# A four-layer graph network on one core: adjacency blocks transposed by DMA, and a reordered first stage

## The chip, the core and the metric

The kernel runs on one core of one Trainium2 chip. Such a core has a matrix engine, TensorE (PE in the profile; its weight loads, PEld, overlap its products), a vector engine (DVE), a scalar engine (ACT), GpSimd (POOL) and SyncE (SP), which here only issues DMAs. ACT and POOL can issue DMAs too; all of them share the core's 16 DMA rings. Every engine works through its own instructions in order and waits for the others by semaphores. The metric is the device time of one execution in microseconds.

## The reference

A node matrix x (3327 x 512) passes four layers that share one adjacency matrix (3327 x 3327, 0/1 integers). Layers 0 to 2 are attention layers with 8, 4 and 8 heads, layer 3 averages over neighbours. Cut to layer 0:

```python
h = jnp.maximum(_layernorm(x, axis=-1), 0.0)
Wh = jnp.einsum('nd,hdo->hno', h, W)                 # 8 heads of 64
f1 = jnp.einsum('hno,ho->hn', Wh, a1)
f2 = jnp.einsum('hno,ho->hn', Wh, a2)
e = leaky_relu(f1[:, :, None] + f2[:, None, :], 0.2)
e = jnp.where(adj[None] > 0, e, NEG_INF)
out = elu(einsum('hnm,hmo->hno', softmax(e, -1), Wh))
x = x + out                                           # heads side by side
```

## The kernel before

Rows are cut into 26 tiles of 128 (the last has 127 rows). Since exp(leaky_relu(f1 + f2)) is a product of a row factor and a column factor on each side of the sign of f1 + f2, attention becomes products of 0/1 matrices with the projected rows, scaled by column factors. For each head and each block of columns a 0/1 matrix "f1 + f2 > 0" is made (`gt`), cut with the adjacency (`tht` = gt AND mask, then `gt` = mask without tht), and both multiply the **pieces** (`ab`): the scaled projected rows, each split into three bf16 parts. The columns come in five groups, `JG` = 6, 6, 6, 4 and 4 blocks of 128. The rows come in seven **chunks** of four tiles (the last of two).

*The first stage* (lines 820 to 847) projects all 26 tiles for layer 0. Tile by tile, `node_stages` gives stages that `Hooks.run` advances by one for each tile in flight: x is loaded, its statistics are taken on DVE, three small steps on POOL end the norm (`norm`), ACT makes the relu (`normed`); PE transposes it and ACT copies it out of PSUM (`transposed`, L137 and L141, tile `hT`); PE projects it (`projected`, L388); ACT and DVE scale and split it (`scaled`, `pieces`); SP stores the pieces to DRAM. The score vectors a1 and a2 are folded into further columns of the weight tile first (`fold`, L299 and L303, half of its products on POOL). From the fifth step on, each step also makes one **mask** (`load_mask`), 20 of them in this stage: POOL loads a 128-row strip of one column group of the adjacency with a cast to bf16 (`at`, L216); PE transposes its blocks into PSUM (`tp`, L221); DVE turns them into 0 or 2 in fp8 (`st`, L225), and SP stores them to DRAM (L230). They are in DRAM since all layers read them again.

*Attention of a layer* (`attention`) runs over the chunks and, for each, over the heads. SP loads the row scores (`s1b`, L624) and the pieces (`ab`, L601: seven buffers, five groups a head); ACT compares 128x512 blocks (L656), DVE some others (L653); DVE makes `tht` and `gt` (L662, L666); PE multiplies in two passes of two row tiles each (L694, L697); DVE reduces. After each pass `hooks.run` lets further work in: the steps of the next layer's tiles, and in layer 0 one or two of the 110 masks that are left. One head before a chunk ends, the masks of the next must be done; SP loads them (L238).

Instructions are placed by a scheduler: on each engine those that are ready go by the order of the program. `after(inst, name)` adds an order to that, without a semaphore. The PSUM tiles `tp` (two buffers) are shared by the masks' transposes and by `transposed`.

Of the kernel before, what the change touches and what calls it, by code (L numbers as in the profile page):

```python
# [52 lines left out]
def tile_gnn(ctx: ExitStack, tc: tile.TileContext, x, adj, W0, a01, W1, al, ar, W2, a2,  # L53
# [95 lines left out]
    stored = {}  # L149
    gone = []  # L150
# [52 lines left out]
    def load_mask(pool, t, g):  # L203


        hooks.done += 1
        n = pn(t)
        c, k = where[t]
        j0, nj = JG[g]
        w = min(nj * P, N - j0 * P)  # L210
        at = pool.tile([P, JM * P], BF16, name="at", bufs=3)
        if n < P:
            nc.vector.memset(at, 0.0)
        elif w < nj * P:
            nc.vector.memset(at[:, w:nj * P], 0.0)
        ld = nc.gpsimd.dma_start(at[:n, :w], adj[t * P:t * P + n, j0 * P:j0 * P + w])  # L216
        if gone:
            after(ld, gone[-2] if len(gone) > 1 else stored[NT - 1])
        tp = ps.tile([P, 8, P], BF16, name="tp", bufs=2)
        for j in range(nj):  # L220
            tr = nc.tensor.transpose(tp[:, j, :], at[:, j * P:(j + 1) * P], identb)  # L221
            if j == 0 and gone:
                after(tr, gone[-1])
        st = pool.tile([P, JM, P], FP8, name="st", bufs=3)
        nc.vector.tensor_scalar(st[:, :nj], tp[:, :nj], 0.0, 2.0, op0=ALU.is_gt, op1=ALU.mult, saturate=False)  # L225
        if j0 <= t < j0 + nj:
            d = pool.tile([P, P], BF16, name="d", bufs=1)
            nc.vector.tensor_tensor(d, tp[:, t - j0, :], negI, ALU.is_gt)
            nc.vector.tensor_scalar(dg1[:, t, :], d, 2.0, None, op0=ALU.mult, saturate=False)
        nc.sync.dma_start(maskd[c][g][:, k], st[:, :nj])  # L230

    def mask_tiles(c, self_loops=False, early=False):
        t0, nt = chunks[c]
        tiles, loops = [], []
        for g, (j0, nj) in enumerate(JG):
            m = mk.tile([P, PER * JM * P], FP8, name="m")
            v = m[:, :nt * nj * P].rearrange("p (k j i) -> p k j i", k=nt, j=nj)
            ld = nc.sync.dma_start(v, maskd[c][g])  # L238
            if early and c == 0:
                after(ld, stored[21])  # L240
            if self_loops:
                for k in range(nt):
                    if j0 <= t0 + k < j0 + nj:
                        loops.append((v[:, k, t0 + k - j0, :].bitcast(U32), dg1[:, t0 + k, :].bitcast(U32)))
            tiles.append(v)
        if self_loops != "later":
            set_loops(loops)
        return (tiles, loops) if self_loops == "later" else tiles
# [14 lines left out]
    def open_layer(l):  # L263
# [17 lines left out]
        for i in range(2):  # L281
            av.append(pre.tile([P, 2, H2, DK], F32, name="h"))
            ld = nc.sync.dma_start(av[i].rearrange("p f h d -> p (f h) d"), a_srcs[l][i].partition_broadcast(P))
            if l:
                after(ld, stored["gate"])
        for k in range(KC):
            for f in range(2):
                dst = L.w[:, k, f, :D // 2]
                if l == 0:
                    nc.sync.dma_start(dst.rearrange("p (g o) -> p g o", g=H2),  # L290
                                      W0[f * H2:(f + 1) * H2, k * P:(k + 1) * P, :].rearrange("h p o -> p h o"))
                else:
                    W = (W1, W2)[l - 1]
                    ld = nc.sync.dma_start(dst, W[k * P:(k + 1) * P, f * (D // 2):(f + 1) * (D // 2)])
                    if l:
                        after(ld, stored["gate"])
        def fold(i, k):
# [3 lines left out]
            if gone:  # L301
                after(m, gone[-1])
            nc.vector.tensor_reduce(L.w[:, k, :, D // 2 + i * H2:D // 2 + (i + 1) * H2], pr, AX.X, ALU.add)  # L303
        folds = [lambda i=i, k=k: fold(i, k) for i in range(2) for k in range(KC)]
        if l:
            hooks.small = folds
        else:
            for f in folds:
                f()
# [18 lines left out]
    def normed(xt, mv, pool, behind=None):  # L328
        h = pool.tile([P, D], F32, name="h", bufs=2)
        act = nc.scalar.activation(h, xt, AF.Relu, bias=mv[:, 3:4], scale=mv[:, 2:3])  # L330
        if behind:
            after(act, behind)
        return h
# [7 lines left out]
    def pieces(L, t, AB, pool, first, behind=None):  # L341
# [32 lines left out]
        elif first and o == two - 1:  # L374
            stored[t] = nc.sync.dma_start(abd[l][g][:, :, js, :].rearrange("h p j w -> p h j w"), pt).ins.name
# [3 lines left out]
    def projected(L, t, hT, first):  # L379
# [4 lines left out]
        pws = []  # L384
        for f in range(2):
            pw = (accs if first else ps).tile([P, D // 2 + H], F32, name="acc" if first else "mm")
            for k in range(KC):
                L.mm = nc.tensor.matmul(pw, hT[:, k, :], L.w[:, k, f, :], start=(k == 0), stop=(k == KC - 1)).ins.name  # L388
# [3 lines left out]
            pws.append(pw)  # L392
# [84 lines left out]
    def node_stages(L, t, get_x, pool, first=False):  # L477
# [30 lines left out]
        if first:  # L508
            return [lambda: (q.update(x=get_x()), statistics(), relu()), turn,
                    lambda: parts(L, t, scaled(L, t, projected(L, t, q["hT"], first), pool, first), pool, first), send]  # L510
# [82 lines left out]
    ahead = {}  # L593

    def load_pieces(L, pool, g, h):
# [4 lines left out]
        v = tl[:, :nj * HW].rearrange("p (j w) -> p j w", j=nj)  # L600
        return v, nc.sync.dma_start(v, abd[L.l][g][h])  # L601

    def attention(L, hooks, open_next, close):
# [4 lines left out]
        masks = mask_tiles(0, l == 1, l == 0)  # L608
        for c, (t0, nt) in enumerate(chunks):
            W = nt * P  # L610
# [3 lines left out]
            for h in range(H):  # L614
# [8 lines left out]
                s1b = rp.tile([P, WMAX], F32, name="s1b", bufs=2)  # L623
                nc.sync.dma_start(s1b[:, :W].rearrange("p (k i) -> p k i", k=nt), s1d[l][t0:t0 + nt, h, :].partition_broadcast(P))  # L624
                ab = []
                for a in range(2 if l == 1 else 1):
                    row = []
                    for g, (_, nj) in enumerate(JG):
# [6 lines left out]
                        else:  # L635
                            v, ld = ahead.pop(g) if g in ahead else load_pieces(L, mp if l else bp, g, h)
# [5 lines left out]
                s1v = s1b[:, :W].rearrange("p (k i) -> p k i", k=nt)  # L642
                th, flip = [[], []], []
                for g, (j0, nj) in enumerate(JG):

                    pt = mp.tile([P, PER * JM * P], FP8, name="tht", bufs=10 if l == 1 else 7)
                    gt = pt if l == 1 else mp.tile([P, PER * JM * P], FP8, name="gt", bufs=7)
                    gv = gt[:, :nt * nj * P].rearrange("p (k j i) -> p k j i", k=nt, j=nj)
                    pv = pt[:, :nt * nj * P].rearrange("p (k j i) -> p k j i", k=nt, j=nj)
                    for jj in range(nj):  # L650
                        j = j0 + jj
                        if j in GP_ON_DVE[l]:
                            nc.vector.tensor_scalar(gv[:, :, jj, :], s1v, L.ns2[:, j, h:h + 1], 2.0,  # L653
                                                    op0=ALU.is_gt, op1=ALU.mult, saturate=False)
                        else:
                            nc.scalar.activation(gv[:, :, jj, :], s1v, AF.Relu, bias=L.ks2[:, j, h:h + 1], scale=BIG,  # L656
                                                 saturate=False)
                    flat = "p k j i -> p (k j i)"
                    mu = masks[g].rearrange(flat).bitcast(U32)
                    gu = gt[:, :nt * nj * P].bitcast(U32)  # L660
                    pu = pt[:, :nt * nj * P].bitcast(U32)
                    nc.vector.tensor_tensor(pu, gu, mu, ALU.bitwise_and)  # L662
                    if l == 1:
                        flip.append((pu, mu))
                    else:
                        nc.vector.tensor_tensor(gu, pu, mu, ALU.bitwise_xor)  # L666
                    th[0].append(pv)
                    th[1].append(gv)
# [109 lines left out]
    def load_x(l, t, pool, *name, behind=None):  # L778
# [7 lines left out]
        if behind:  # L786
            after(ld, behind)
# [32 lines left out]
    with tc.tile_pool(name="first", bufs=1) as fp:  # L820
# [5 lines left out]
        def first_x(t, lead=6):  # L826

            while len(xa) < min(NT, t + lead):
# [4 lines left out]
                nc.sync.dma_start(xt[:pn(u)], x_rows(0, u))  # L833
# [5 lines left out]
        hooks.masks = [lambda t=t, g=g: load_mask(ip, t, g) for t in range(NT) for g in range(len(JG))]  # L839
        hooks.tiles = [node_stages(L, t, lambda t=t: first_x(t), fp, True) for t in range(NT)]  # L840
        n = 0
        while hooks.tiles or hooks.flying:
            hooks.run(1, 0, 1 if n >= 4 and hooks.done < 20 else 0)
            for g, (j0, nj) in enumerate(JG[:-1]):
                if n == j0 + nj + 2:
                    ahead[g] = load_pieces(L, bp, g, 0)
            n += 1
    A, R = [("A", D, F32, n) for n in A_BUFS], ("R", PER * 2 * 129, F32, 1)
    ab, gt, tht = ("ab", JM * 400, BF16, 7), ("gt", PER * JM * P, FP8, 7), ("tht", PER * JM * P, FP8, 7)
    tags = [[A[0], R, tht, ("gap", 15 * 1024, FP8, 1), gt],  # L850
            [A[1], ("ab", JM * 258, F32R, 7), R, ("ts", 2 * JM * P, F32R, 3), ("tv", 2 * 4 * P, F32R, 2), tht[:3] + (10,)],
            [A[2], ab, ("R", PER * 2 * 65, F32, 1), tht, gt]]
    hooks.masks = [lambda t=t, g=g: load_mask(ip, t, g) for t in range(NT) for g in range(len(JG))][hooks.done:]
# [531 lines left out]
```

## Time and profile before

| | us |
|---|---|
| four timed runs | 3610.37, 3605.89, 3600.28, 3607.64 |
| their median | 3606.77 |
| the profiled execution | 3605.24 |
| its span, first to last instruction | 3603.3 |
| PE busy | 3466.8 (96%) |
| DVE, ACT, POOL busy | 2648.8, 2511.2, 602.3 |
| first attention product of layer 0 starts | 180.92 |
| last adjacency transposes start | 990.6 |

Line numbers (L221) are those of the kernel before. A busy time is the sum of an engine's records; matmuls are pipelined, so that a record of 0.25 us may follow another after 0.08 us, and what a matmul costs is read from the distance of starts. A wait is an engine's idle time, with the instruction that ended it. The ring share is the mean busy share of the 16 DMA rings. SPq lines are DMAs that SP issues. Durations come from one profiled execution, of which only the order and the distances are used.

### The profile page before, as it was taken

How to read it: one execution, taken by the hardware profiler on the slowest of the kernel's cores; microseconds unless marked ns; L12 is line 12 of the kernel's file. 1: busy time of each engine (PE TensorE's matmuls, PEld its weight loads, DVE VectorE, ACT ScalarE, POOL GpSimd, SP SyncE). 2: the span in 40 equal slices, each digit the busy share in tenths (PEclk: the TensorE clock that was granted, in tenths of full speed). 3: DMA queues.
4: the chain of work that ended last, by engine and by line, in shares of the span. 5: the costliest groups of instructions: out<-in, count | busy, mean ns of one | idle time of the engine just before them, and what ended most of it. 6: DMA issues, size and time to landing. Idle time of an engine off the chain costs nothing. (4 is left out here: it accounts for less than half of the span.)

```text
span 3603.3 us, 78551 instructions
## 1 busy us (share of the span) xinstructions
PE 3466.8 (96%) x31291; PEld 3129.6 (87%) x31291; DVE 2648.8 (74%) x5227; ACT 2511.2 (70%) x4113; POOL 602.3 (17%) x855
## 2 busy tenths in 40 slices
PE   6799999999999999999999989999999999999998
PEld 5599999999999878888888869989898989876886
DVE  6698888888887779888888868867676768672211
ACT  5688787777787788888798767767676767572111
POOL 6501221111110111233222230001010101010000
PEclk9899999999999999999999999999999999999999
DMA  7688787788766877877777876655555555576331
GB/s 211 220 237 229 202 230 210 220 220 234 228 205 208 283 274 262 288 253 276 279 259 271 312 268 201 195 178 183 176 187 182 172 176 189 167 271 253 102 104 52
DMA packets 369431, 780.69 MB, mean 217 GB/s; under 512 B 35906, under 2 KB 207333, under 8 KB 368416
## 3 DMA queue, kind: packets, MB, share of 16 engines
q1 hardware_dynamic: 341024, 713.17, 59.5%
q0 software_dynamic: 28032, 62.41, 7.2%
q8 instruction: 249, 4.08, 0.4%
q14 instruction: 126, 1.03, 0.1%
HBM read 667.96 MB, written 129.64 MB: 221 GB/s over the span
## 5 line engine op out<-in xcount | busy, mean ns | idle before, releaser
L694 PE MATMUL acc<-ab,tht 128*128 128x195 bf16 (+1 forms) x10816 | 1840.1, 248 | 14.9 <-DVE tht L662 13.6
L697 PE MATMUL acc<-ab,gt 128*128 128x195 bf16 (+1 forms) x10816 | 1839.1, 248 | 6.5 <-DVE rc L734 3.9
L656 ACT ACTIVATE gt<-s1b,ks 128x512 fp8e4<-128x512 f32 (+1 forms) x2464 | 1457.3, 677 | 315.3 <-issue 158.5
L694 PEld LDWEIGHTS <-tht 128*128 128x128 fp8e4 x10816 | 1059.0, 98 | 28.2 <-DVE tht L662 15.2
L697 PEld LDWEIGHTS <-gt 128*128 128x128 fp8e4 x10816 | 1058.7, 98 | 26.5 <-issue 19.8
L662 DVE TENSOR_TENSOR tht<-gt,m 128x768 uint32<-128x768 uint32 (+3 forms) x560 | 446.7, 798 | 141.5 <-ACT gt L656 139.5
L666 DVE TENSOR_TENSOR gt<-tht,m 128x768 uint32<-128x768 uint32 (+3 forms) x560 | 450.1, 804 | 8.7
L590 ACT CAST ts<-tht 128x1536 fp32r<-128x1536 fp8e4 x208 | 300.1, 1470 | 59.0 <-PE acc L687 55.7
L687 PE MATMUL acc<-ab,ts 128*128 128x258 f32 x2496 | 334.1, 290 | 4.6 <-ACT ts L590 3.4
L653 DVE TENSOR_SCALAR gt<-s1b,ns 128x512 fp8e4<-128x512 f32 (+1 forms) x448 | 221.9, 500 | 148.7 <-PE acc L697 147.5
L687 PEld LDWEIGHTS acc<-ab,ts 128*128 128x128 f32 x2496 | 313.9, 190 | 13.6 <-ACT ts L590 3.8
L921 PE MATMUL acc<-y,mf 128*128 128x512 f32 x1352 | 309.8, 391 | 1.6 <-DVE mf L916 1.6
L656 ACT ACTIVATE tht<-s1b,ks 128x512 fp8e4<-128x512 f32 (+1 forms) x504 | 308.5, 681 | 2.8 <-DMA s1b<-s 2.3
L921 PEld LDWEIGHTS acc<-y,mf 128*128 128x128 f32 x1352 | 253.5, 188 | 57.8 <-DVE mf L916 2.0
L712 DVE TENSOR_REDUCE R<-acc 128x130 f32<-128x390 f32 x416 | 214.2, 554 | 91.8 <-PE acc L697 91.2
L797 POOL TENSOR_TENSOR xt<-xt,e 128x512 f32<-128x512 f32 x72 | 123.2, 1711 | 888.9 <-DVE e L796 578.8
L690 PE MATMUL acc<-ab,tht 128*128 128x387 bf16 x1248 | 225.8, 329 | 7.6 <-DMA ab<-ab 4.8
L918 ACT CAST mf<-m 128x768 fp32r<-128x768 fp8e4 (+1 forms) x78 | 59.1, 762 | 245.1 <-PE acc L921 233.3
L687 PE MATMUL acc<-ab,tv 128*128 128x258 f32 x1664 | 219.4, 283 | 2.7 <-DVE R L708 0.9
L687 PEld LDWEIGHTS acc<-ab,tv 128*128 128x128 f32 x1664 | 207.3, 189 | 5.1 <-DVE tv L590 1.6
L388 PE MATMUL mm<-w,hT 128*128 128x260 f32 (+1 forms) x832 | 199.0, 393 | 9.9 <-ACT hT L141 6.2
L690 PEld LDWEIGHTS <-tht 128*128 128x128 fp8e4 x1248 | 117.3, 98 | 84.7 <-DMA ab<-ab 5.2
(141 smaller groups left out, 3412.1 us busy)
## 6 DMA issues: line engine op xcount, KB each, us to landing
ab<-ab SPq DMA_DIRECT2D x336, 600.0 KB, 5.6
ab<-ab SPq DMA_DIRECT2D x224, 400.0 KB, 4.0
ab<-ab SPq DMA_DIRECT2D x112, 774.0 KB, 6.2
ab<-ab SPq DMA_DIRECT2D x112, 516.0 KB, 5.4
ab<-ab SPq DMA_DIRECT2D x56, 582.0 KB, 6.1
s1b<-s SPq DMA_DIRECT2D x120, 256.0 KB, 6.1
m<-mask SPq DMA_DIRECT2D x72, 384.0 KB, 4.0
ab<-pt SPq DMA_DIRECT2D x13, 1600.0 KB, 7.6
```

The costliest lines, as they stand in the source:

```text
L388: L.mm = nc.tensor.matmul(pw, hT[:, k, :], L.w[:, k, f, :], start=(k == 0), stop=(k == KC - 1)).ins.name
L590: (nc.scalar.copy if KIND[g] == "s" else nc.vector.tensor_copy)(t[:, :k1 - k0, :nj], th[a][g][:, k0:k1])
L653: nc.vector.tensor_scalar(gv[:, :, jj, :], s1v, L.ns2[:, j, h:h + 1], 2.0, op0=ALU.is_gt, op1=ALU.mult, saturate=False)
L656: nc.scalar.activation(gv[:, :, jj, :], s1v, AF.Relu, bias=L.ks2[:, j, h:h + 1], scale=BIG, saturate=False)
L662: nc.vector.tensor_tensor(pu, gu, mu, ALU.bitwise_and)
L666: nc.vector.tensor_tensor(gu, pu, mu, ALU.bitwise_xor)
L687: mm = nc.tensor.matmul(acc[k][:, :2 * DA], thr[g][:, k - ks[0], jj, :], ab[a][g][:, jj, :], start=(j == 0), stop=(j == NT - 1), skip_grou ...
L690: mm = nc.tensor.matmul(acc[k][:, :3 * DA], th[a][g][:, k, jj, :], ab[a][g][:, jj, :3 * DA], start=(j == 0), stop=(j == NT - 1), skip_grou ...
L694: nc.tensor.matmul(acc[k][:, :3 * DA + o], th[0][g][:, k, jj, :], ab[0][g][:, jj, :3 * DA + o], start=(j == 0), stop=False, skip_group_che ...
L697: mm = nc.tensor.matmul(acc[k][:, AO:AO + 3 * DA + o], th[1][g][:, k, jj, :], ab[0][g][:, jj, AO:AO + 3 * DA + o], start=False, stop=(j == ...
L712: nc.vector.tensor_reduce(R[:, k], v.rearrange("p a (s d) -> p a d s", s=3), AX.X, ALU.add)
L921: nc.tensor.matmul(acc[k], mf[:, jj, :], y2[g][:, jj, s, :], start=(j0 + jj == 0 and s == 0), stop=(j0 + jj == NT - 1 and s == 1))
```

## The change

The masks of row tiles 0 to 3 (20 of 130) are still transposed on PE, in the first stage, now group by group; DVE writes them straight into the tiles that chunk 0 of layer 0 uses (`masks0`), beside the store to DRAM. The masks of tiles 4 to 25 (110) are transposed by DMA, on SP's queue, from `at` to a new tile `tr` in SBUF. Their three steps (load, turn, compare) are spread over three calls: each call loads one mask, turns the one before and compares the one before that.

In the first stage, x tiles from the third on, a2 and half of W are loaded on ACT's queue; the folds follow the first two tiles' relus; tiles 0 and 1 are projected without the folded columns first and get those later (`products`); head 0's pieces are copied from SBUF into `ab` and not loaded from DRAM; and the 0/1 matrices of groups 0 to 2 for head 0 of chunk 0 are made a step at a time during the projections (`matrices`, in buffers that are free then).

```diff
-    def load_mask(pool, t, g):
...
-        tp = ps.tile([P, 8, P], BF16, name="tp", bufs=2)
-        for j in range(nj):
-            tr = nc.tensor.transpose(tp[:, j, :], at[:, j * P:(j + 1) * P], identb)
...
+    def mask_steps(pool, t, g):
...
+        def load():
+            at = q["at"] = pool.tile([P, JM * P], BF16, name="at", bufs=3)
...
+            ld = nc.gpsimd.dma_start(at[:n, :w], adj[t * P:t * P + n, j0 * P:j0 * P + w])
+            after(ld, gone[-1] if gone else relus[-3])
+
+        def turn():
+            at = q["at"]
+            if c == 0:
+                tp = q["tp"] = ps.tile([P, 8, P], BF16, name="tp", bufs=2)
+                for j in range(nj):
+                    nc.tensor.transpose(tp[:, j, :], at[:, j * P:(j + 1) * P], identb)
+            else:
+                tp = q["tp"] = mp.tile([P, JM, P], BF16, name="tr", bufs=3)
+                tr = nc.sync.dma_start(tp[:, :nj], at[:, :nj * P], transpose=True)
+                after(tr, gone[-1] if gone else stored[NT - 1])
+
+        def compare():
+            hooks.done += 1
+            tp = q["tp"]
+            if c == 0:
+                st = masks0[g][:, k]
+            else:
+                st = pool.tile([P, JM, P], FP8, name="st", bufs=3)[:, :nj]
+            cm = nc.vector.tensor_scalar(st, tp[:, :nj], 0.0, 2.0, op0=ALU.is_gt, op1=ALU.mult, saturate=False)
+            if gone:
+                after(cm, gone[-1])
...
+            nc.sync.dma_start(maskd[c][g][:, k], st)
+        return load, turn, compare
...
-            ld = nc.sync.dma_start(av[i].rearrange("p f h d -> p (f h) d"), a_srcs[l][i].partition_broadcast(P))
+            ld = (nc.sync if l or i == 0 else nc.scalar).dma_start(av[i].rearrange("p f h d -> p (f h) d"),
...
-                    nc.sync.dma_start(dst.rearrange("p (g o) -> p g o", g=H2),
+                    (nc.scalar if f else nc.sync).dma_start(dst.rearrange("p (g o) -> p g o", g=H2),
...
-            if gone:
-                after(m, gone[-1])
+            if gone or i:
+                after(m, gone[-1] if gone else relus[1])
...
+            if g not in ahead:
+                ahead[g] = pieces_tile(L, bp, g)
+            nc.sync.dma_start(ahead[g][:, js], pt[:, 0])
...
+    def products(L, pws, hT, o, e):
+        for f, pw in enumerate(pws):
+            for k in range(KC):
+                mm = nc.tensor.matmul(pw[:, o:e], hT[:, k, :], L.w[:, k, f, o:e], start=(k == 0), stop=(k == KC - 1))
...
+    def matrices(L, nt, h, g, s1v, mask, pt, gt):
...
+        def compare(jj):
+            j = j0 + jj
+            if j in GP_ON_DVE[l]:
+                nc.vector.tensor_scalar(gv[:, :, jj, :], s1v, L.ns2[:, j, h:h + 1], 2.0,
+                                        op0=ALU.is_gt, op1=ALU.mult, saturate=False)
+            else:
+                nc.scalar.activation(gv[:, :, jj, :], s1v, AF.Relu, bias=L.ks2[:, j, h:h + 1], scale=BIG,
+                                     saturate=False)
+
+        def split():
+            nc.vector.tensor_tensor(pu, gu, mu, ALU.bitwise_and)
+            if l != 1:
+                nc.vector.tensor_tensor(gu, pu, mu, ALU.bitwise_xor)
...
-                nc.sync.dma_start(xt[:pn(u)], x_rows(0, u))
+                ld = (nc.scalar if u > 1 else nc.sync).dma_start(xt[:pn(u)], x_rows(0, u))
+                if relus:
+                    after(ld, relus[-1])
...
+        for n in range(2):
+            hooks.run(1, 0, 0)
+        for f in folds:
+            f()
         while hooks.tiles or hooks.flying:
+            n += 1
             hooks.run(1, 0, 1 if n >= 4 and hooks.done < 20 else 0)
...
+            if n == 7:
+                early["s1"] = score_rows(0, 0, PER, 0)
+            for g in range(3):
+                if n == (8, 15, 21)[g]:
...
+                    pv, gv, _, steps = matrices(L, PER, 0, g, early["s1"], masks0[g], b[:, :s], b[:, s:2 * s])
+                    hooks.small += steps
+                    early[g] = pv, gv
...
+    steps = [mask_steps(ip, t, g) for t, g in order[20:]]
+    for i in range(len(steps) + 2):
+        hooks.masks.append(lambda ss=[steps[i - s][s] for s in range(3) if 0 <= i - s < len(steps)]: [s() for s in ss])
```

## The prediction

> **What bounds the kernel now.** I read the page's head first, then busy time by stretches of the run that I cut at the stages, then TensorE's (PE's) waits inside two of them, then the order of instructions around one adjacency transpose.
>
> ```profile
> span 3603.3 us, 78551 instructions
> PE 3466.8 (96%) x31291; PEld 3129.6 (87%) x31291; DVE 2648.8 (74%) x5227; ACT 2511.2 (70%) x4113; POOL 602.3 (17%) x855
> ```
>
> The profiled execution took 3605.24 us (span 3603.3 and 1.9 around it); the median of the four timed runs is 3606.77, so I work on the profiled one and add 1.5 at the end. PE is the bound on the average. The table by stretch (busy us of PE, PEld, DVE, ACT, POOL with counts; then granted clock, busy share of the DMA rings, GB/s) shows where it is not:
>
> ```profile
> 0.00:31.50 31.50, 11.58 (x48) 9.21 (x48) 19.68 (x46) 8.94 (x17) 19.51 (x47) 0.99 0.69 177
> 31.50:172.40 140.90, 114.75 (x583) 93.94 (x583) 95.11 (x197) 89.95 (x196) 84.89 (x140) 0.92 0.74 224
> 172.40:184.50 12.10, 3.06 (x19) 2.52 (x20) 8.81 (x15) 10.26 (x18) 5.27 (x7) 0.58 0.79 242
> 184.50:1150.00 965.50, 950.49 (x10882) 934.98 (x10880) 816.26 (x1613) 758.31 (x1281) 147.44 (x231) 1.00 0.75 218
> 1000.00:1090.00 90.00, 90.00 (x1018) 88.85 (x1016) 73.80 (x149) 75.48 (x129) 15.15 (x18) 1.00 0.62 194
> ```
>
> The first three rows are the first stage (projection of 26 row tiles, then the start of attention): 55 of 184.5 us without PE. The fourth is layer 0's attention, 98% PE. The fifth is a piece of it after the last adjacency transpose: PE without a gap, rings down from 0.75 to 0.62. PE's waits, first stage and then layer 0's attention (total us, times, longest):
>
> ```profile
> PE acc L388 <- ACT hT L141: 27.7, 21, 11.2
> PE tp L137 <- ACT h L330: 16.2, 1, 16.2
> PE acc L694 <- DVE tht L662: 8.6, 1, 8.6
> ...
> PE tp L221 <- ACT hT L141: 6.9, 8, 1.4
> PE tp L221 <- DMA at<-in_adj_dram: 4.1, 2, 3.8
> PE tp L221 <- ACT s1t L474: 1.4, 2, 1.1
> ```
>
> In layer 0 nearly all of PE's waiting, 12.4 us, stands before L221, the transposes that the change removes: they share the two "tp" buffers with the projection's transposes, and PE works in order. What a transpose costs PE beside that is read from starts, not from its 219 ns record, since matmuls overlap:
>
> ```profile
> 315.53 0.25 PE L697 MATMUL acc<-ab,gt 128*128 128x195 bf16 x1
> 315.61 0.72 PE L221 MATMUL tp<-identb,at 128*128 128x128 bf16 x10
> 316.17 0.25 PE L694 MATMUL acc<-ab,tht 128*128 128x195 bf16 x1
> ```
>
> Ten transposes push the next product back by 0.56 us: 0.056 us each.
>
> **Part 1: the transposes.** Of 676 blocks of 128x128, those of the first four row tiles (104) stay on PE, in the first stage; 572 go, all in layer 0's attention, which PE bounds. 572 x 0.056 = 32 us on the path, and the 12.4 us of waits go with them: -44. A page of the Trainium skill prices this differently ("TensorE: Matmul & The Clock Gate", Part 4: PE-mode transpose: about 275 ns in one kernel's context); by that it would be 157 us, and the step of 56 ns in this trace decides against it.
>
> What comes instead: 110 transposing DMAs (22 row tiles x 5 column groups) on SP's queue, SBUF to SBUF, 4 or 6 blocks each. No row shows a transposing DMA. Lower bound of its ring time: the 321 GB/s that the rings moved while busy (780.69 MB in 67.4% of the span), 0.10 us a 32 KB block, 58 us in all. Nearest row for short rows: the load of layer 0's W, whose rows are 256 bytes (64 floats a head), had the rings to itself between 5 and 8 us: share 1.02, 206 GB/s; at that rate a block of 128 rows of 256 bytes is 0.16 us, 91 us in all. Upper bound: each such row costs what a packet of SP's queue costs on average (341024 packets in 59.5% of 16 engines' span: 0.10 us), so 128 x 0.10 / 16 = 0.80 us a block, 460 us in all. I take 91 us, as W's rows are nearest in size. Free ring time in layer 0's attention is 0.25 x 965 = 241 us, so 91 fits.
>
> The Trainium skill speaks on both sides here, and no run shows which holds. "VectorE: DVE Perf Modes", The three transpose paths, gives a 128x128 bf16 block 1309 ns by DMA against 390 ns on TensorE; end to end that would be an estimated 749 us, far over the free ring time. "Advanced Engine Details and Errata", X-Bar Transpose (TRN2), has transposing DMAs as fast as regular ones, 350-400 GB/s, an estimated 54 us.
>
> What stands behind them on SP's queue is the loads of pieces (L601, median 5.2 us to landing). A pass of one head is 26 x 2 x 2 products at 0.0835 us = 8.7 us. Seven buffers hold five groups of a head, so the third group's load goes out when the running head's first is done, 6/26 into its second pass, and is used 12/26 into the next pass: 8.7 x 32/26 = 10.7 us, so 5.5 us to spare. PE never waited on "ab" here. A transpose waits on SP for its "at" (median 5.8 us, longest 9.3), but is meant to be issued a mask later than the load; I price the delays that get through, together with DVE's compare waiting for the transposed tile in DVE's order (it held DVE 3 us for PE before), at 5 us, between 0 and 44 (0.4 us for each of 110). SP has the time: 275.7 us of L601's waits in 200 to 1150 are for buffers. Its issue cost is between 0.32 us (a mask store) and 1.17 us (an x load in the 8.20 us row of seven), at most 129 us. DVE's compare reads SBUF in place of PSUM: at most the 0.84 us of now; DVE is 85% busy, ACT 79%, so 4% less PE time leaves both under. Chunk 0's masks are no longer read back (1.8 MB) and head 0's pieces are copied from SBUF in place of read: nothing, both hidden. Net of part 1: -39.
>
> **Part 2: the first stage.** Start. The first transpose starts at 16.2 us since POOL's three small steps of the norm (2.0 us) stood behind its W multiply until 10.6. With the folds behind the second relu they run from 5.1, when the statistics are done: 5.1 + 2.0, relus 1.5, transpose and copy 1.6: products from 10, when W (waited on until 8.7) is there. Both tiles' wide products took 8.9 us; the narrow ones are bounded by PEld's 0.2 us x 32 records = 6.5. So tile 2 starts at 25.4 and not at 31.5: -6, and its products lose the slow 6.83 us (others 3.83) that followed the 3 us gap: take -8, between -4 and -11.
>
> Middle, 31.5 to 172.4: 24 tiles at PE's step of 4.94 us would be 119 of 141 us. The largest wait is this:
>
> ```profile
> 117.70 0.17 DVE L322 BATCH_NORM_AGGREGATE mv<-st 128x2 f32<-128x6 f32 x1
> 128.32 0.69 DVE L318 BATCH_NORM_STATS2 st<-xt 128x6 f32<-128x512 f32 x1 [10.45 <-DMA xt<-in_x_dram]
> ```
>
> It is the last x tile (127 rows), issued on SP at 114.51; DVE stood on it and PE lost 11.2 us. On ACT's queue it goes out behind relu 19, which here ran at 116.35: no earlier, so I keep the stall, and count its 11 us as the good end. The other x waits on DVE sum to 13 us, of which PE felt some 3. What is added: 16 compares x 0.677 = 10.8 us and 24 issues x 0.32 to 1.17 = 8 to 28 us on ACT, which has 141 - 90 = 51 us free; 6 splits x 0.85 and 2 compares x 0.5 = 6 us on DVE, which has 46. Covered in sum, but not at every tile: 0 to 10 us, I take 3. Net 0.
>
> End. PE waited 8.6 us for the first matrices, and ran the first 28 products at half the step (180.9 to 184.5, against 2.3 us). Three of five groups, 18 of 26 columns, are now ready before the projections end, 6 us of products, while ACT makes the rest: -9, between -5 and -10.
>
> Net of part 2: -17, between +1 and -32. Nothing else in the program changes in amount.
>
> **Sum**: 3605.2 - 39 - 17 = 3549; on the median, 3551. Own range of this case 3525 to 3580.
>
> **The rivals.**
> - A: the first stage gives nothing (ACT, now with issues in its order, holds the projection back). For it: ACT's hT copy already ends PE's waits 21 times. Against: 51 us free. 3607 - 39 = 3568.
> - B: attention gives its gain back: PE loses the L221 waits and meets as many behind late masks, DVE or pieces. For it: DVE works in order, 85% busy, and now waits for a DMA. Against: two steps of distance, three buffers. 3607 - 17 = 3590.
> - C, slower: the transposing DMAs saturate the rings in layer 0's attention, and loads of pieces behind them on SP's queue come late, so PE waits in each head. For it: 0.75 of the rings is taken already, and no row shows how such a DMA moves. It decides from 241 / 572 = 0.42 us a block on. At the upper bound layer 0 takes 724 + 460 = 1184 us in place of 965, +219: with part 2's gain some 3809.
>
> **How the numbers follow.** The forecast gets 0.48, A 0.12, B 0.12, C 0.24, no change 0.04. A measurement of this kernel can tell about 0.2% (7 us). Faster: 0.48 + 0.12 + 0.12 = 0.72. The range 3522 to 3630 holds the forecast, A, B, no change and the beginning of C, and leaves out most of C (0.19) and 0.01 below.
>
> **What would show it.** Right: L221 with 104 matmuls, none after the first stage; in layer 0's attention PE at 99% or more with no "ab" among its waits, rings at 0.80 to 0.88; attention starting near 166 us and layer 0 ending some 55 us earlier; all later stages as long as now. Part 2 wrong: tile 2 later than 28 us, or more than 5.2 us a tile with ACT full. Part 1 wrong: PE waiting on "ab", or on "tht" behind DVE waiting for the transposed tile; a transposing DMA that lands after 10 us or more; rings at 1. The forecast falls with more than 0.42 us of rings a block.

## The result, and the profile after

The changed kernel takes 3611.19 us (median of 36 runs, 3600.52 to 3623.46) against 3608.46 of the kernel before (57 runs): ratio 1.0007, 95% interval 1.0002 to 1.0013. It is some 2.5 us slower, which is within what counts as no change here; 3551 had been forecast. The profiled execution took 3613.33 us, span 3611.1. In what follows, line numbers are those of the kernel of which a view is shown; the changed kernel has the transposing DMA at L231, the comparison at L241, the operation on the diagonal tile at L246, the pieces at L707 and the products of attention at L753 and L756.

The page's head, and the DMA totals, which were 369431 packets, 35906 of them under 512 bytes:

```profile
span 3611.1 us, 77633 instructions
...
PE 3445.5 (95%) x30751; PEld 3103.9 (86%) x30751; DVE 2616.1 (72%) x5227; ACT 2508.9 (69%) x4113; POOL 611.3 (17%) x855
...
DMA packets 446598, 797.70 MB, mean 221 GB/s; under 512 B 112690, under 2 KB 285781, under 8 KB 445584
```

PE has 540 fewer matmul records and 21 us less busy time, and the run is no shorter: PE stands idle instead. Where, the same stretches show as before (PE, PEld, DVE, ACT, POOL, then clock, ring share, GB/s):

```profile
0.00:31.50 31.50, 19.18 (x90) 16.33 (x91) 18.71 (x44) 8.97 (x17) 17.00 (x44) 0.89 0.54 146
31.50:172.40 140.90, 111.18 (x567) 91.13 (x566) 104.64 (x203) 96.61 (x207) 89.45 (x139) 0.93 0.73 214
172.40:184.50 12.10, 12.10 (x133) 11.62 (x132) 5.07 (x13) 9.51 (x19) 4.45 (x5) 1.00 0.88 313
184.50:1150.00 965.50, 912.06 (x10142) 890.37 (x10140) 777.45 (x1604) 748.72 (x1266) 155.03 (x238) 0.99 0.94 237
1000.00:1090.00 90.00, 90.00 (x1017) 88.85 (x1015) 75.88 (x153) 79.42 (x135) 14.42 (x18) 1.00 0.66 207
```

Up to 184.5 us PE has 142.5 us of work in place of 129.4. In layer 0's attention (fourth row) it has 912 in place of 950: 53 us idle where it was 15, and the rings are at 0.94 in place of 0.75. After the last mask (fifth row) PE is as before. PE's waits in the fourth stretch (total us, times, longest), where L221's 12.4 us had been nearly all:

```profile
PE acc L753 <- DMA ab<-ab: 18.2, 10, 3.1
PE acc L753 <- DVE tht L661: 12.1, 12, 3.8
PE acc L756 <- DVE gt L663: 8.4, 9, 1.9
PE acc L756 <- DVE dg L247: 6.9, 1, 6.9
```

PE waits for pieces, and for DVE, and DVE for the transposing DMAs:

```profile
DVE st L241 <- DMA tr<-at: 64.0, 25, 8.3
...
DVE d L246 <- DMA tr<-at: 32.6, 12, 5.4
```

Among the DMA issues of the page the line is `tr<-at SPq DMA_TRANSPOSE x110, 6.5` (median us to landing; 2.9 to 11.4 us). The first of them shows how the waits come about: SP's order, then DVE's, then PE's.

```profile
200.79 2.98 SPq L231 DMA_TRANSPOSE tr<-at  x2
```

```profile
207.12 0.56 DVE L241 TENSOR_SCALAR st<-tr 128x768 fp8e4<-128x768 bf16 x1 [8.31 <-DMA tr<-at]
207.59 0.28 DVE L246 TENSOR_TENSOR d<-tr,negI 128x128 bf16<-128x128 bf16 x1
...
207.87 0.95 DVE L663 TENSOR_TENSOR gt<-tht,m 128x768 uint32<-128x768 uint32 x1
```

```profile
208.97 0.48 PE L756 MATMUL acc<-ab,gt 128*128 128x195 bf16 x2 [6.92 <-DVE dg L247]
```

The DMA goes out on SP at 200.79. DVE's next instruction in order is its comparison, so DVE stands for 8.31 us with `gt` of head 1 behind it, and PE stands for 6.92 us because that `gt` is missing. The stall costs more than its length: PE's products then start 0.16 us apart until 212.3 in place of 0.084, with a granted clock of 0.67 from 200 to 210 us and 0.89 from 210 to 220 (1.00 in both before).

By ends of heads (DVE's reciprocal in the last step of a head, L794, L735 before): head 0 of chunk 0 ends at 208.9 (217.3 before), head 1 at 234.0 (229.5), head 0 of chunk 1 at 371.9 (358.9), head 0 of chunk 5 at 1029.9 (1024.3). The lead of 8 us is gone within head 1, and 13 us are missing by the first head of the second chunk, of which some come back later.

### The profile page after: what moved, and what is told of

Its sections match the earlier page's. It is cut to its first block, busy times and chain, and to the rows that moved or that the text cites. A ratio compares the mean times of both kernels' runs of the same rounds, so it can differ in the third digit from the quotient of the medians.

```text
span 3611.1 us, 77633 instructions
## 1 busy us (share of the span) xinstructions
PE 3445.5 (95%) x30751; PEld 3103.9 (86%) x30751; DVE 2616.1 (72%) x5227; ACT 2508.9 (69%) x4113; POOL 611.3 (17%) x855
## 3 DMA queue, kind: packets, MB, share of 16 engines
q14 instruction: 129, 1.06, 0.1%
## 5 line engine op out<-in xcount | busy, mean ns | idle before, releaser
L753 PE MATMUL acc<-ab,tht 128*128 128x195 bf16 (+1 forms) x10744 | 1828.2, 248 | 37.9 <-DMA ab<-ab 19.5
L756 PE MATMUL acc<-ab,gt 128*128 128x195 bf16 (+1 forms) x10744 | 1825.9, 248 | 27.7 <-DVE gt L663 10.5
L756 PEld LDWEIGHTS <-gt 128*128 128x128 fp8e4 x10744 | 1052.2, 98 | 74.6 <-issue 44.8
L753 PEld LDWEIGHTS <-tht 128*128 128x128 fp8e4 x10744 | 1052.3, 98 | 34.4 <-DVE tht L661 21.3
```

The source lines that it names most:

```text
L753: nc.tensor.matmul(acc[k][:, :3 * DA + o], th[0][g][:, k, jj, :], ab[0][g][:, jj, :3 * DA + o], start=(j == 0), stop=False, skip_group_che ...
L756: mm = nc.tensor.matmul(acc[k][:, AO:AO + 3 * DA + o], th[1][g][:, k, jj, :], ab[0][g][:, jj, AO:AO + 3 * DA + o], start=False, stop=(j == ...
```

## The experiments

Times are medians; ratios are to the kernel before on the same chip, with 95% intervals. "us against before" is (ratio - 1) x 3608. The interval of one such figure is about 3 to 5 us either way, that of a difference between two experiments 5 to 7.

**1. Part 2 alone.** All masks transposed on PE again, each in one call; the changed first stage stays.

```diff
-            if c == 0:
+            if True:
                 tp = q["tp"] = ps.tile([P, 8, P], BF16, name="tp", bufs=2)
...
-        hooks.masks.append(lambda ss=[steps[i - s][s] for s in range(3) ...
+    hooks.masks = [lambda ss=ss: [s() for s in ss] for ss in steps]
```

> The changed kernel with all 130 masks transposed on PE again, each made in one call as before the change: the first stage's part alone. Theory 1 (order): a compare that stands right behind its transposing DMA holds DVE, which held tht and gt back and PE with them; theory 2 (rings): the packets of the transposing DMAs fill the rings and every load comes late. Both expect the first stage's gain to stay here, as no transposing DMA is left: attention starts 7 us earlier as in the changed kernel, the 6.9 us stall at 202 us is gone, total 3595 to 3603 against 3608 before. If the first stage's gain is lost for a reason of its own (ACT and DVE late for head 1), 3605 to 3610.

3608.75 us, ratio 0.9999 (0.9990 to 1.0008). The changed first stage is worth nothing by itself, within some 3 us. The first attention product starts at 176.4 in place of 180.9, head 0 ends at 217.4 (217.3): the lead ends at PE's transposes of the fifth tile's masks, whose adjacency has not landed.

```profile
198.47 0.51 PE L228 MATMUL tp<-identb,at 128*128 128x128 bf16 x6 [3.84 <-DMA at<-in_adj_dram]
200.16 0.82 PE L228 MATMUL tp<-identb,at 128*128 128x128 bf16 x6 [1.18 <-DMA at<-in_adj_dram]
203.15 0.51 PE L751 MATMUL acc<-ab,tht 128*128 128x195 bf16 x2 [1.96 <-DVE tht L659]
```

**2. More distance.** The comparison three masks after the load in place of two (the transposing DMA stays one behind), five `tr` tiles.

```diff
-    for i in range(len(steps) + 2):
-        ... ss=[steps[i - s][s] for s in range(3) ...
+    late = (0, 1, 3)
+    for i in range(len(steps) + late[2]):
+        ... ss=[steps[i - late[s]][s] for s in range(3) ...
```

> The changed kernel with each compare two masks later than now (three masks behind its transposing DMA's turn less one: load i, turn i-1, compare i-3; five tr buffers for three), so that no compare shares a call with its own transposing DMA. The DMAs are the same. Theory 1 (order): DVE's 97 us of waits for tr in 200 to 1000 us fall under 25, PE's idle time there falls by 20 to 35 us: total 3575 to 3592. Theory 2 (rings): DVE waits less, but PE then waits for ab or tht as long as before: total 3605 to 3615, ring share still 0.95 or more.

3591.39 us, 0.9962 (0.9949 to 0.9975). One hook may run two entries of the list, so that in the changed kernel "two masks later" can be the next instruction. DVE's waits at the comparison fall from 64.0 to 2.9 us. What is left has moved to two other readers or writers of the same data:

```profile
DVE d L246 <- DMA tr<-at: 47.3, 15, 6.4
...
DVE at L219 <- DMA tr<-at: 11.3, 3, 5.7
...
DVE at L217 <- DMA tr<-at: 5.6, 3, 2.5
...
DVE st L241 <- DMA tr<-at: 2.9, 1, 2.9
```

**3 and 4. No wait for the DMAs; no DMAs.** In both, the comparison reads `at` itself, so the masks of tiles 4 to 25 are left untransposed and only the times can be compared. In the first the transposing DMAs still run, in the second they are gone.

```diff
-            tp = q["tp"]
+            tp = q["tp"] if c == 0 else q["at"].rearrange("p (j i) -> p j i", j=JM)
...
-                tr = nc.sync.dma_start(tp[:, :nj], at[:, :nj * P], transpose=True)   # in 4 alone
```

> The changed kernel with DVE's compare of tiles 4 to 25 reading at in place of tr: the transposing DMAs are all issued, but nobody waits for them (layer masks of these tiles are left untransposed). Theory 1 (order): PE's idle time in layer 0's attention falls to about 20 us, total 3570 to 3585. Theory 2 (rings): with the rings as full as before, loads of pieces still come late, total 3600 to 3612.

> As the kernel whose compare reads at, and without the 110 transposing DMAs (the masks of tiles 4 to 25 are left untransposed): what is to be had at most from taking the transposes off PE. Both theories: ring share in layer 0's attention back to 0.75, no ab among PE's waits, total 3560 to 3572. The distance to the kernel that issues the DMAs and waits for none is the rings' price: under 10 us by theory 1, 30 us or more by theory 2.

3590.74 us, 0.9966 (0.9955 to 0.9976), and 3575.85 us, 0.9908 (0.9895 to 0.9922). The DMAs cost about 21 us by the ratios (0.0058 x 3608; 15 by the medians) when nobody waits for their data. That is rings and buffers together: POOL still waits 47.1 us for `at` buffers that a transposing DMA reads. Both theories hold a part, DVE's order and the DMAs themselves. The order shows without them too: DVE's operation on the diagonal tile now waits for the adjacency load, 54.7 us in all and 43.4 in the second.

**5 to 8. The missing gain of the first stage, and the distance again.** Three masks of distance helped; would four help more? And is the first stage's lead lost at the last x tile (127 rows; DVE waits 10.6 us for it here, 10.45 before), or at the switch, behind layer 1's weights on SP?

```diff
+                for a, b in ((0, pn(u)),) if pn(u) == P else ((0, 112), (112, pn(u))):        # 5, 8
-                ld = (nc.scalar if u > 1 else nc.sync).dma_start(xt[:pn(u)], x_rows(0, u))
+                    ld = (nc.scalar if u > 1 else nc.sync).dma_start(xt[a:b], x_rows(0, u)[a:b])
...
-                if c == 0 and h == 1:                                                          # 6, 8
+                if c == 0 and h == 3:
                     stored["gate"] = ld.ins.name
                     N_ = open_next()
...
+    late = (0, 2, 4)                                                                           # 7, 8
```

> The changed first stage with every mask transposed on TensorE (as in the first experiment, 3608.75 us), and the last x tile (127 rows) loaded by two DMAs of 112 and 15 rows. Theory T, the gain of the first stage is lost at the last x tile: without the 10.5 us wait of its statistics attention starts 8 to 11 us earlier, near 165, and the end comes as much earlier, 3597 to 3602 us. Theory S, the gain is lost at the switch, in head 0 and head 1, where TensorE then waits for the adjacency load of the fifth mask and for the pieces of head 1 behind the weights of layer 1: attention starts earlier here too, but the end of head 1 stays within 2 us of 232.8 and the time within 3 us of 3608.75.

3596.41 us, 0.9968 (0.9956 to 0.9979). Theory T: the split is worth 11 us and the end comes as much earlier. No wait of DVE for an x tile after 100 us is longer than 2.0 us now.

> The changed first stage with every mask transposed on TensorE, and the ten loads of layer 1's weights (8 us of issues on SP, from 192 to 202 us) moved from head 1 to head 3 of the first chunk. Theory S: the hole of 8.6 us on TensorE between 194.6 and 203.1 shrinks below 3 us, the end of head 1 comes near 225, and the time is 3600 to 3604 us. Theory T: the weights were not in the way; head 1 ends within 2 us of 232.8 and the time is 3606 to 3611 us.

3610.79 us, 1.0013 (1.0004 to 1.0022). Theory S has head 1 right, which ends 6 us earlier (226.7), and the total wrong: the first head of the sixth chunk still ends 5.5 us earlier (1023.4 against 1028.9), but the end comes no earlier. Where the 5.5 us go after that was not followed.

> The change with more distance between a mask's three steps: the load in one hook, the transposing DMA two masks later, the comparison four masks later (against one and two in the change, one and three in the second experiment, which ran in 3591.39 us). If what is left of the DVE waits there (47 us before the diagonal's operation, which first reads the transposed tile) is order, it goes and the time is 3580 to 3587 us; if it is the rings' time of 650 to 1000 us alone, the time stays at 3588 to 3594 us.

3601.60 us, 0.9988 (0.9976 to 0.9999): worse than a distance of three, which neither theory had. The adjacency tile has three buffers. With the turn two masks after the load, the load of a mask needs the buffer that was turned a moment ago. That is read from the waits, and no run with more buffers tests it: POOL's loads wait longer, and DVE's clearing of the padding in the same buffer (L217, L219) waits 33 us in place of 17:

```profile
POOL at L220 <- DMA tr<-at: 309.4, 45, 18.2
```

It is 222.0 us in experiment 2.

> The distance of two and four masks, the last x tile by two DMAs, and layer 1's weights at head 3, together. If the three act on different waits, the time is that of the kernel with the distance alone less 5 to 15 us: 3572 to 3585 us. If the switch into attention is bound by its data (pieces, scores and adjacency on full rings) whatever the order, it is within 3 us of the kernel with the distance alone.

3603.88 us, 0.9993 (0.9984 to 1.0003). Head 1 ends 15 us ahead of experiment 7's (216.8 against 232.0), the sixth chunk's first head 1.5 us ahead. Here, too, late masks seem to eat an earlier start.

**9 to 12. The order of the other readers.** In experiment 2's trace the diagonal's operation of the first such mask stands at 206.31, its comparison at 217.34. Only the comparison had an order given to it (`after(cm, gone[-1])`); the other was placed ahead of it.

```diff
-                nc.vector.tensor_tensor(d, tp[:, t - j0, :], negI, ALU.is_gt)
+                dd = nc.vector.tensor_tensor(d, tp[:, t - j0, :], negI, ALU.is_gt)      # 9 to 12
+                after(dd, cm.ins.name)
...
-                nc.vector.memset(at, 0.0)
+                (nc.gpsimd if gone else nc.vector).memset(at, 0.0)                        # 10 to 12
...
+    the last x tile as 112 and 15 rows                                                    # 11, 12
...
-            if c == 0:
+            if c == 0 or g % 2:                                                           # 12
                 tp = q["tp"] = ps.tile([P, 8, P], BF16, name="tp", bufs=2)
```

> The second experiment's order (transposing DMA one mask after the load, comparison three masks after it; 3591.39 us) with one more order: the operation on the diagonal tile, the second reader of the transposed mask, stands behind its mask's comparison on VectorE instead of up to 8 us ahead of it. Theory D, the 47 us that VectorE still waited for a transposing DMA there were order and not ring time: those waits fall below 10 us and the time to 3578 to 3587 us. Theory R, full rings (0.95 to 1.04 from 200 to 1000 us) set the pace whatever the order on VectorE: 3588 to 3594 us, the waits turning up elsewhere.

3584.71 us, 0.9943 (0.9929 to 0.9956).

> As the run before it, and the clearing of the padding of the adjacency tile, on which VectorE waited 17 us for the transposing DMA that still read the tile's buffer, moved from VectorE to GpSimd. Theory D: 2 to 8 us less than the run before it. Theory R: within 2 us of it.

3579.13 us, 0.9934 (0.9921 to 0.9948). Theory D's numbers, for both; the step from experiment 9 to 10 (3 us by the ratios) lies within the interval, and the waits speak for it. DVE's waits for transposing DMAs are down from 96.6 us to this, in the same stretch:

```profile
DVE st L241 <- DMA tr<-at: 4.4, 1, 4.4
```

> As the run before it, and the last x tile by two DMAs of 112 and 15 rows, which gave 12 us where TensorE transposes (3608.75 to 3596.41). Theory D: the 10 to 13 us of the earlier start of attention stay: 3566 to 3578 us. Theory R: with full rings the lead of the start is lost again over the first four chunks, as it was with the distance of two and four masks (14 us ahead at the end of head 1, 1.5 at the end of chunk 4); the time is within 4 us of the run before it.

3573.08 us, 0.9907 (0.9894 to 0.9921), the profiled one with span 3569.4: 0.93% faster than the kernel before. The 10 us of the start stay now that the masks are in time.

> As the run before it, but of the masks after the fourth tile every second column group is transposed on TensorE (55 of 110, 0.056 us a block, some 15 us of TensorE in all), so that the rings carry half of the transposing DMAs. Theory R: the rings fall from about 1.0 to about 0.9, the stalls go, and the time is 3565 to 3580 us, below the run before it by 3 us or more. Theory D: the run before it has no stalls left to lose, and this one is 10 to 20 us slower than it for the 15 us of TensorE.

3575.61 us, 0.9912 (0.9898 to 0.9926). Neither theory's number. The edit moves 44 masks to PE, turned in the call that compares them, and not 55, as two of the five column groups have an odd number; 66 transposing DMAs are left. The rings go down to 0.90 and PE's waits for pieces from 17.1 to 3.7 us, while 220 blocks on PE (12 us at 0.056) and longer waits for DVE's `tht` and `gt` (16.3 us in place of 9.7) take back as much.

**13 to 16. What was still open.** The split alone on the changed kernel; the two orders without the distance; the rings' price in the right order; the split alone on the kernel before.

```diff
   changed kernel + the last x tile as 112 and 15 rows                               # 13
   changed kernel + after(dd, cm.ins.name) + memset of at on GpSimd                  # 14
   as 14, the comparison reads at, no transposing DMAs                               # 15
   kernel before + the last x tile as 112 and 15 rows                                # 16
```

> The changed kernel with the last x tile loaded by two DMAs of 112 and 15 rows, nothing else. If the waits of the attention are waits for the transposing DMA's completion, whose issue moves with the start, the 12 us gained with TensorE transposing come here too: 3597 to 3602 us. If VectorE's waits set the pace of the first four chunks whatever the start, as with the distance of two and four masks, most of it is lost again: 3606 to 3612 us.

3602.25 us, 0.9986 (0.9975 to 0.9996): 8 of the 11 us.

> The changed kernel with its own distances (load, transposing DMA one mask later, comparison two masks later), the diagonal's operation behind its mask's comparison and the padding cleared by GpSimd. If distance is the larger part, VectorE still waits at the comparison (64 us before) and the time is 3598 to 3606 us; if the order of the second reader was, 3582 to 3592 us.

3603.05 us, 0.9987 (0.9977 to 0.9997). The waits only gather at the first reader:

```profile
DVE st L241 <- DMA tr<-at: 66.3, 32, 7.1
```

Distance and order both count: order alone gives 7 us, distance alone 16, together 26 (experiments 14, 2 and 10 against the changed kernel); that this is more than their sum lies within the interval.

> The run that put the diagonal's operation and the padding in order (3579.13 us with the comparison three masks after the load), without the transposing DMAs: the comparison reads the untransposed adjacency tile, so the masks of all but the first four tiles are left untransposed; load, nothing, comparison two masks later. The rings go from about 1.03 to about 0.78. If the rings cost 15 us as they did in the order of the change (3590.74 against 3575.85), 3562 to 3567 us; if rings at 1.0 cost little once nobody waits for one DMA, 3570 to 3578 us.

3562.63 us, 0.9864 (0.9850 to 0.9878). The masks are left untransposed, as in experiment 4. Against experiment 10, 0.0070 x 3608 = 25 us (interval some 7 either way) is what the DMAs cost with the order right. The two profiled executions lie 14 us apart, so the size is uncertain; one mask less of distance is in it, too. Layer 0's attention with them (experiment 10), then without:

```profile
184.50:1150.00 965.50, 940.20 (x10478) 923.42 (x10476) 802.28 (x1635) 769.79 (x1317) 170.96 (x268) 0.99 0.97 246
```

```profile
184.50:1150.00 965.50, 952.01 (x10638) 935.25 (x10636) 815.88 (x1672) 790.34 (x1364) 177.34 (x277) 0.99 0.78 232
```

The ring share differs by 0.19 of 965.5 us, 183 us for 572 blocks: 0.32 us a block. That is an estimate: the packets of other loads may take longer, too, when the rings are full. PE's waits with them are mostly for DMAs and what stands behind one; the longest wait for `gt` follows 7.73 us in which DVE waited for a load of scores:

```profile
PE acc L754 <- DMA ab<-ab: 10.5, 7, 3.7
PE acc L757 <- DVE gt L664: 9.6, 4, 6.2
```

Without them, `ab` holds PE for 0.8 us in all.

> The kernel before, with the last x tile loaded by two DMAs of 112 and 15 rows, nothing of the change. Its trace has 11.2 us of waiting there. If the later steps take the start as it comes, 8 to 12 us faster, 3594 to 3599 us; if head 0's masks and pieces are late behind it anyway, within 3 us of before.

3597.36 us, 0.9969 (0.9958 to 0.9980). The split is worth 11 us without any of the change, as much as with it (experiment 5: 0.9968). So the first stage's own changes are worth nothing clear of noise with the split either.

**17 and 18. The early 0/1 matrices.** Experiments 5 and 11 without them.

```diff
-            for g in range(3):
+            for g in range(0):
                 if n == (8, 15, 21)[g]:
```

> The changed first stage with every mask transposed on TensorE and the last x tile by two DMAs (3596.41 us), without the early 0/1 matrices of groups 0 to 2: they are made at the start of attention as in the kernel before. Theory E, the early matrices cost the projections what they save at the switch: the 15 tiles from the eleventh to the last take 77 to 80 us in place of 88, the last projection ends 8 to 10 us earlier, TensorE waits 8 us for the first matrices again, and the time is within 3 us of 3596.4. Rival F, the lead is lost to something else in the stage (SP, rings, x on ACT's queue): the tiles still take 85 us or more, and with the wait back at the switch the time is 3602 to 3607 us.

3599.04 us, 0.9976 (0.9967 to 0.9985). Mixed: the time is within 3 us as theory E has it, but the last projection starts at 160.1, not earlier than with them (159.3). They do not slow the projections. They save 10 us at the first product (163.0 against 173.0), of which 3, within the interval, are left at the end.

> The fastest version so far (3573.08 us: distances one and three, the diagonal's operation and the padding in order, the last x tile by two DMAs) without the early 0/1 matrices. Theory E: within 3 us of 3573. Rival F: 3578 to 3584 us.

3572.12 us, 0.9901 (0.9886 to 0.9916): no difference from experiment 11 (0.9907). Theory E's number, though its reason is refuted by the run before.

## Why the prediction was wrong, step by step

**-44 for what leaves PE: right.** Between experiments 1 and 15, which differ by the transposes and their waits (and 15 by the two orders), lie 0.0135 x 3608 = 49 us, some 6 either way. Between experiments 1 and 4 it is 33, since 4 still has the changed kernel's order on DVE. The 44 lie between the two. Where a page of the Trainium skill would have had 157 us ("TensorE: Matmul & The Clock Gate", Part 4), the 0.056 us read from the distance of starts held.

**Ring price, 0.16 us a block: mis-sized, 0.32, and held against the wrong free time.** The nearest row had been the load of W, whose short rows are 256 bytes. The size of the packets was right: experiment 3 has 76736 more packets of under 512 bytes than experiment 4, which differs by these DMAs alone, and 572 x 128 = 73216 of them are the blocks' rows. The price was not, and neither was the room: the 241 us were counted over 965 us, of which the last 158 have no transposing DMA. From 200 to 1000 us the rings were at 0.76 to 0.78 before. That leaves some 180 of 800 us, and 183 us fill them. The rows from 600 to 800 us, of the kernel before, of experiment 10 and of experiment 15:

```profile
600.00:800.00 200.00, 193.77 (x2186) 189.99 (x2185) 164.08 (x325) 152.21 (x259) 30.88 (x52) 0.99 0.78 218
```

```profile
600.00:800.00 200.00, 196.35 (x2156) 192.55 (x2154) 168.61 (x344) 160.98 (x273) 34.06 (x58) 0.99 1.06 256
```

```profile
600.00:800.00 200.00, 200.00 (x2243) 197.14 (x2241) 171.89 (x348) 164.01 (x280) 34.24 (x55) 1.00 0.84 243
```

The share is a sum of packets' times and can pass 1; in experiment 10 it is 1.02 to 1.06 from 200 to 1000 us, so the rings are full there, and the 0.97 is an average with a stretch in which they are not. Rival C's limit of 0.42 us a block, worked out from the same 241 us, is some 0.32 over that stretch, just what a block took. Its mechanism is there, its price is not: loads of pieces and scores come late here and there, and the DMAs cost 25 us in all, where C had 219 at its upper bound. "It fits" had been taken for "it costs nothing". Two pages of the Trainium skill bear on this. Transposes as fast as regular DMAs ("Advanced Engine Details and Errata", X-Bar Transpose (TRN2)) do not agree with these runs: 32 KB in 0.32 us of ring time is an estimated 102 GB/s, where all transfers of the kernel before had 321. 1309 ns a block ("VectorE: DVE Perf Modes", The three transpose paths), added up end to end, would be four times the 183 us; no run here times one block alone.

**Delays, 5 us (0 to 44): the step that failed.** They were 51 us, from experiment 15 to the changed kernel: 25 that the DMAs cost even in the right order, for which the prediction had nothing beyond these 5, and 26 that experiment 10 takes away with the same work (one operation on another engine, two more `tr` tiles). The prediction took the code's "a mask later" for a distance in time. It is a distance in a list, of which one hook may run two entries. It also asked only when the comparison waits, and not about the other instructions that touch the same tiles: the diagonal's operation and the clearing of `at`. That is rival B, "meets as many behind late masks, DVE or pieces", which had 0.12 and a price of 3590, since it kept part 2's 17 us. Of the gain of part 1 nothing is left, as B has it.

**Start, -8: -1.8.** The first projection starts 7.0 us earlier (18.0 to 11.0), and tile 2 at 29.7 in place of 31.5; 25.4 was forecast, and later than 28 was to show part 2 wrong. The forecast moved the folds behind the second relu and did not ask what they then stand in front of: tile 2's norm, on DVE and POOL.

```profile
19.14 0.69 DVE L325 TENSOR_REDUCE w<-e 128x8 f32<-128x512 f32 x1 [1.38 <-POOL e L321]
19.74 0.68 DVE L335 BATCH_NORM_STATS2 st<-xt 128x6 f32<-128x512 f32 x1
21.20 0.69 DVE L325 TENSOR_REDUCE w<-e 128x8 f32<-128x512 f32 x1 [0.78 <-POOL e L321]
21.80 0.17 DVE L339 BATCH_NORM_AGGREGATE mv<-st 128x2 f32<-128x6 f32 x1
```

The folds' product has one buffer (`e`), so POOL and DVE take turns at 2.07 us a fold until 21.9. Tile 2's relu starts at 23.34 (22.94 before). PE is done with the first two tiles at 25.3, as forecast; but tile 2's transposes start only there, at 25.16, and its products follow them by 4.5 us (4.1 before). The forecast had no time for these between the tiles.

**Middle, 0: +4.0.** From tile 2 to tile 25, 136.5 us before and 140.5 after, within the 0 to 10 that the ACT additions had. With the last x tile split on both sides it is 122.0 and 129.9. The early matrices, which were the suspect, are not it (130.3 without them). In the traces about half of the 7.9 us is PE's idle time (20.9 us against 16.6, summed over windows of 2 us), and the rest a lower granted clock (0.96 against 0.99 from 30 to 153 us). What makes PE idle there stays open.

**End, -9: -9.2, and given back.** From the start of the last projection to the first product it is 3.7 us in place of 12.9. The forecast stopped there. The next thing due is the fifth tile's mask, and PE loses 7 us to it: 6.9 behind DVE's diagonal in the changed kernel, 7.0 in the three rows of experiment 1. The prediction had not named what is late next.

**The sum.** 3549 had -39 and -17. Measured: -49 + 51 for part 1, 0 for part 2.

## What to carry to other kernels

When work moves from an engine to a queue, ask for each instruction that reads or rewrites the moved data where it stands in its engine's order, and count its distance to the producer in us of the running kernel, not in loop steps; an order given to one reader does not hold for the other. Count a resource's free time over the stretch in which the new load runs, not over the whole stage, and price a transfer by what is due behind it. A stage that starts or ends earlier is worth what the next due item allows: follow the lead to the first instruction that waits again, and only then count it.

## What was not expected of the hardware

- A transposing DMA within SBUF runs as rows of 256 bytes: 572 blocks are 73216 rows and 18.74 MB, and experiment 3 has 18.8 MB more than experiment 4; an estimated 0.32 us of 16 rings for a block of 128x128 bf16; 6.5 us from issue to landing for 4 or 6 blocks with rings near full (2.9 at least). SP needs 1.33 us (median; 5.25 at most) to issue one, against 0.59 for the load of scores and 0.33 for the mask store behind the first of them.
- DVE waited 10.5 us for the last x tile, of 127 rows; in the last 2 us of that wait the rings' share was 0.07, about one of 16, at 27 GB/s. Loaded as 112 and 15 rows it is there in time, for 11 us of the total. The Trainium skill ("DMA: Bandwidth & Descriptors", Why a DMA increments its semaphore by 16 and not by 1) has a DMA spread over the largest number of engines up to 16 that divides its outer size, so that 127 rows go through one. The runs agree with it: one ring is busy, 112 divides by 16, and with the split the wait goes. The prediction had taken that wait for a late issue and kept it.
- The comparison of a 128x768 tile in bf16 takes 0.58 us from SBUF and 0.95 from PSUM (means in the changed kernel's trace).
